# Moving the output stores of a last stage out of the load queue

## The chip, the cores and the metric

The kernel runs on one core of a Trainium2 chip. The metric is the device time of one execution in microseconds (us), the median of three runs. A core has a matrix engine (TensorE, in the profile PE), three elementwise engines (VectorE or DVE, ScalarE or ACT, GpSimd or POOL) and SyncE (SP), which here does nothing but issue DMA transfers. Each engine works through its own instruction stream in order and waits on semaphores. ScalarE can issue DMA transfers too. All transfers between the chip's main memory (HBM) and the on-chip memory (SBUF) are carried out by the same 16 DMA engines of the core.

## The reference

The input `x` has 384 channels of 192 x 192 pixels in float32 (56.6 MB). Two layers, each with a residual, are computed; cut to what matters:

```python
def gn(v):                      # group norm over 32 groups of 12 channels
    ...
def layer0(x):                  # channel attention
    qkv = max_pool_2x2(w_qkv @ x + b_qkv)        # 1152 channels of 96 x 96
    q, k, v = split(depthwise_3x3(qkv) + b_dw)
    attn = normalized(q) @ normalized(k).T       # 8 heads, 48 x 48
    out = sum(a_i * topk_softmax(attn, k_i) @ v) # four values of k
    return w_proj @ repeat_2x2(gelu(out)) + b_proj
def layer1(x):                  # binary convolution with a shift per channel
    xb = sign(x)
    shifted = shift_columns(xb, dx(channel))     # -3 .. 3 columns
    return sign(weight) @ shifted + bias
x = x + layer0(gn(x))
x = x + layer1(gn(x))           # only the sign of gn(x) is needed: x - mean
```

The second layer needs the group means of the whole result of the first, so its pass over the image can start only when the attention of the first layer is done everywhere.

## The kernel before

The image is cut into 24 units of 8 rows (NU = 24), each `[128 partitions, 3 channel tiles, 1536]` float32, 2304 KB. Three passes run over all units: statistics; q and k with their Gram matrix; then v, whose depthwise result stays in six on-chip `chunk` buffers of four units each, with the attention applied in place. The change concerns only what comes after them, the last stage. For every unit it adds the projected attention to `x` in place (`summed`), takes the signs of the result (`signed`, with GpSimd copies that complete the column shifts, `moved`), multiplies them by the sign weights, adds that to `x` in place too and stores the unit (`finished`). Line numbers of the profile stand beside the lines.

```python
def unit(u, pool=big, parts=1):
    xt = pool.tile([P, CT, UPX], F32, name="xt", tag="big")    # CT = 3 channel tiles
    n = CT // parts
    for t in range(0, CT, n):
        nc.sync.dma_start(xt[:, t : t + n], xv[u][:, t : t + n])              # L176
    return xt

def projected(ps, u, m):                # one of three channel tiles
    ...                                 # 6 matmuls on PE                       L493
    for r in range(2):                  # adds them to xt[:, m] in place, DVE   L502
        nc.vector.scalar_tensor_tensor(x5[:, m, r], yb, bpr[:, m : m + 1], x5[:, m, r], ALU.add, ALU.add)

# ... last stage
order = [...]                           # 19, 18, 23, 17, 16, 22, 21, 20, 15, 14, ...
left = [UC] * NCH                       # units that still need each chunk (4 each)
todo = [u for u in order if u not in kept]     # units to load; kept: three are there

def summed(i):
    u = order[i]
    if i >= len(FIRST):                 # the first two were done earlier
        for m in range(CT):
            projected(pyp.tile([P, PPX], F32, name="yps"), u, m)
    left[u // UC] -= 1
    if not left[u // UC] and todo:      # a chunk is done with: its buffer takes a unit
        v = todo.pop(0)
        kept[v] = unit(v, parts=CT)

def signed(i):
    xt, sg = kept[order[i]], signs[i % NSIGN]          # NSIGN = 3
    for t in range(CT):
        for h in range(2):
            ...
            nc.scalar.activation(rows_of(sg, ...), xt[p, t, :]..., AF.Sign, bias=nmean1[...])  # L655
            moved(sg, t, h)             # GpSimd copies                         L633 to L647

def finished(i):
    u = order[i]
    xt, sg = kept.pop(u), signs[i % NSIGN]
    v = todo.pop(0) if todo else None

    def load(m):                        # the next unit, into the same buffer
        if v is not None:
            nc.sync.dma_start(xt[:, m], xv[v][:, m])                          # L673

    for m in range(CT):
        for r0 in range(0, UR, 4):
            ...                         # 6 matmuls on PE                       L680
            nc.vector.scalar_tensor_tensor(blk, ps[...], bl1[...], blk, ALU.add, ALU.add)     # L688
        nc.sync.dma_start(ov[u, :, m], xt[:, m])                              # L691
        if m:
            load(m - 1)
    load(CT - 1)
    if v is not None:
        kept[v] = xt

with tc.manual_schedule():              # instructions go out in this order
    v = todo.pop(0)
    kept[v] = unit(v, more, parts=CT)
    for i in range(3):
        summed(i)
        if i < 2:
            signed(i)
    for i in range(NU):
        if i == 0:
            summed(3)
        elif i > 1 and i + 2 < NU:
            summed(i + 2)
        if i + 2 < NU:
            signed(i + 2)
        finished(i)
```

So SyncE's stream holds, for each unit, store 0, store 1, load 0, store 2, load 1, load 2, each of 768 KB. A load overwrites the third that was just stored, so it waits until that store has landed. At the start of the stage the units have four buffers: eight of the pool less six chunks, and two made for this stage (`early`, `more`). A fifth comes free with the fifth unit, and more as further chunks are done with.

Of the kernel before, what the change touches and what calls it, by code (L numbers as in the profile page):

```python
# [15 lines left out]
AF = mybir.ActivationFunctionType  # L16
# [6 lines left out]
CT = C // P  # L23
# [9 lines left out]
NU = H // UR  # L33
# [9 lines left out]
HALF = P // 2  # L43

STEP = 1584
SAT = [16 + t * STEP + t - SHIFT // 2 for t in range(CT)]
SALL = SAT[-1] + SLEN + PITCH + 9
REST = 32
NSIGN = 3
# [29 lines left out]
def shift_halves():  # L79

    dx = lambda c: (c % SHIFT + SHIFT // 2) % SHIFT - SHIFT // 2
    of = {d: [c for c in range(C) if dx(c) == d] for d in range(-(SHIFT // 2), SHIFT // 2 + 1)}
    shift = [[t - SHIFT // 2, t + 1] for t in range(CT)]
    other = []
    at = np.zeros((P, CT), int)
    for t in range(CT):
        other.append([])
        for h, (d, e) in enumerate(zip(shift[t], (shift[t][1], 0))):  # L90
            n = HALF - len(of[d])
            at[h * HALF : (h + 1) * HALF, t] = of[d][:REST] + of[e][:n] + of[d][REST:]
            of[e] = of[e][n:]
            other[-1].append((e, n))
    assert sorted(at.flat) == list(range(C))
    return at, shift, other


XCH, HSHIFT, OTHER = shift_halves()
# [43 lines left out]
def conv_preact_kernel(ctx: ExitStack, tc: tile.TileContext, a: dict, out: bass.AP):  # L143
    nc = tc.nc
    xv = a["x"].rearrange("u t p n -> u p t n")
    ov = out.rearrange("u t p n -> u p t n")
# [10 lines left out]
    parts = {name: small[:, i:j] for name, i, j in SMALL}  # L157
# [7 lines left out]
    nmean1 = const.tile([P, CT], F32, name="nmean1")  # L165
# [6 lines left out]
    def unit(u, pool=big, parts=1):  # L172
        xt = pool.tile([P, CT, UPX], F32, name="xt", tag="big")
# [4 lines that stand above are left out]
# [36 lines left out]
    kept = {}  # L214
    with tc.tile_pool(name="p1", bufs=1, side="right") as p1, tc.tile_pool(name="p1ps", bufs=2, space=PSUM) as psp:
# [5 lines left out]
        for i in range(NU):  # L221
            u = NU - 1 - i
            xt = unit(u, parts=CT if u in (0, NU - 1) else 1)
# [13 lines left out]
            else:  # L237
                b, k = divmod(seen, BATCH)
# [105 lines left out]
    with tc.tile_pool(name="p2w", bufs=1, side="right") as wp, tc.tile_pool(  # L344
# [7 lines left out]
        for u in range(NU):  # L352
            xt = kept.pop(u) if u in kept else unit(u)
            lo, hi = rows(u)
            n = hi - lo + 1
# [128 lines left out]
    def opened(name, bufs, **kw):  # L484
        return end.enter_context(tc.tile_pool(name=name, bufs=bufs, reuse_waits="tile", **kw))

    def projected(ps, u, m):

        xt = kept[u]
        o = chunk[u // UC][:, :, u % UC * PPX : (u % UC + 1) * PPX]  # L490
        x5 = xt.rearrange("p t (i a j b) -> p t a i j b", a=2, b=2, j=WP)
        for t in range(CT):
            nc.tensor.matmul(  # L493
                ps,
                wpr[:, t, m * P : (m + 1) * P],
                o[:, t, :],
                start=(t == 0),
                stop=(t == CT - 1),
            )
        yb = ps.rearrange("p (i j) -> p i j", j=WP).unsqueeze(3).to_broadcast([P, PR, WP, 2])  # L500
        for r in range(2):
            nc.vector.scalar_tensor_tensor(x5[:, m, r], yb, bpr[:, m : m + 1], x5[:, m, r], ALU.add, ALU.add)  # L502

    chunk = []
    with ExitStack() as vs:
# [39 lines left out]
        for u in range(NU):  # L545
            xt = unit(u)
# [9 lines left out]
            for m in range(CT):  # L556
                parts = []
# [39 lines left out]
    with end:  # L597
        more, sp = opened("p5x1", 1), opened("p5s", 1)
        pyp, psp = opened("p5py", 2, space=PSUM), opened("p5ps", 3, space=PSUM)
        signs = [sp.tile([P, SALL], F8, name=f"signs{i}") for i in range(NSIGN)]  # L600

        rest = [sp.tile([P, SLEN], F8, name=f"rest{i}") for i in range(2)]
        assert SALL % 4 == LEAD % 4 == PITCH % 4 == W % 4 == 0
        for ts in (*signs, *rest):
            nc.gpsimd.memset(ts.bitcast(F32), 0.0)

        def rows_of(ts, p, at=0, pitch=PITCH, n=W):
            return ts[p, at : at + UR * pitch].rearrange("p (r w) -> p r w", w=pitch)[:, :, :n]

        order = [u for c in reversed(range(NCH)) for u in reversed(range(c * UC, (c + 1) * UC))]  # L610
        ahead = [*FIRST, NU - 1, *(u for u in order if u // UC == FIRST[0] // UC and u not in FIRST)]
        order = [*ahead, *(u for u in order if u not in ahead)]
        left = [UC] * NCH
        todo = [u for u in order if u not in kept]

        def summed(i):

            u = order[i]
            if i >= len(FIRST):
                for m in range(CT):  # L620
                    projected(pyp.tile([P, PPX], F32, name="yps"), u, m)
            left[u // UC] -= 1
            if not left[u // UC] and todo:
                v = todo.pop(0)
                kept[v] = unit(v, parts=CT)

        def moved(sg, t, h):

            d, n = OTHER[t][h]
            p = slice(h * HALF + REST, h * HALF + REST + n)  # L630
            src, to = SAT[t] - HSHIFT[t][h], SAT[t] - d
            by = rest[t % 2]
            nc.gpsimd.tensor_copy(  # L633
                rows_of(by.bitcast(I32), p, 0, PITCH // 4, W // 4),
                rows_of(sg.bitcast(I32), p, src // 4, PITCH // 4, W // 4),
            )
            if d:

                assert to % 4 == 0
                nc.gpsimd.tensor_copy(sg.bitcast(I32)[p, to // 4 : (to + SLEN) // 4], by.bitcast(I32)[p])  # L640
            elif to % 2 == 0:
                nc.gpsimd.tensor_copy(
                    rows_of(sg.bitcast(U16), p, to // 2, PITCH // 2, W // 2),
                    rows_of(by.bitcast(U16), p, 0, PITCH // 2, W // 2),
                )
            else:
                nc.gpsimd.tensor_copy(rows_of(sg, p, to), rows_of(by, p))  # L647

        def signed(i):

            xt, sg = kept[order[i]], signs[i % NSIGN]
            for t in range(CT):
                for h in range(2):
                    p = slice(h * HALF, (h + 1) * HALF)
                    nc.scalar.activation(  # L655
                        rows_of(sg, p, SAT[t] - HSHIFT[t][h]),
                        xt[p, t, :].rearrange("p (r w) -> p r w", w=W),
                        AF.Sign,
                        bias=nmean1[p, t : t + 1],
                        saturate=False,  # L660
                    )
                    moved(sg, t, h)

        def finished(i):


            u = order[i]
            xt, sg = kept.pop(u), signs[i % NSIGN]
            v = todo.pop(0) if todo else None

            def load(m):
                if v is not None:
                    nc.sync.dma_start(xt[:, m], xv[v][:, m])  # L673

            for m in range(CT):
                for r0 in range(0, UR, 4):
                    ps = psp.tile([P, 2, 512], F32, name="l1ps")
                    for j in range(2):
                        for t in range(CT):
                            nc.tensor.matmul(  # L680
                                ps[:, j, : 2 * W],
                                wb[:, t, m * P : (m + 1) * P],
                                rows_of(sg, slice(0, P), SAT[t])[:, r0 + 2 * j : r0 + 2 * j + 2],
                                start=(t == 0),
                                stop=(t == CT - 1),
                            )
                    blk = xt[:, m, r0 * W : (r0 + 4) * W].rearrange("p (j n) -> p j n", j=2)
                    nc.vector.scalar_tensor_tensor(  # L688
                        blk, ps[:, :, : 2 * W], bl1[:, m : m + 1], blk, ALU.add, ALU.add
                    )  # L690
                nc.sync.dma_start(ov[u, :, m], xt[:, m])  # L691
                if m:
                    load(m - 1)
            load(CT - 1)
            if v is not None:
                kept[v] = xt

        with tc.manual_schedule():
# [8 lines that stand above are left out]
                    summed(3)  # L707
                elif i > 1 and i + 2 < NU:
                    summed(i + 2)
                if i + 2 < NU:  # L710
                    signed(i + 2)
                finished(i)


# [70 lines left out]
```

## Time and profile before

| | |
|---|---|
| device time, median of three | 2373.09 us (2371.77 to 2376.79) |
| the profiled execution | 2368.62 us, of which the profile spans 2366.8 us |
| PE busy | 2155.2 us, 91% of the span |
| DVE busy | 1825.2 us, 77% |
| ACT busy | 878.2 us, 37% |
| read from HBM, written | 213.68 MB, 56.62 MB |
| share of 16 DMA engines, SyncE's queue | 30.4% |

The profile page is of one execution. It gives the busy time of each engine, the span in 40 slices (a digit is a share in tenths, a last row the GB/s that the DMA engines moved), the chain of work that ended last, groups of instructions with the mean time of one, and the DMA issues with the median time from issue to landing. Answers about a window of time are read in the same way: "windows" gives the busy time of every engine, the number of instructions, the granted clock of PE, the busy share of the DMA engines and their GB/s in each window; "timeline" gives instructions in order of time, merged into runs (start, length, engine, line, operation). A DMA-issuing instruction stands in SyncE's timeline as `SPq`; a run of them includes what they waited for in between. Most of the span, up to about 2012 us, is bound by PE in the three passes and is the same in both kernels; the last 350 us are the stage of the change.

### The profile page before, as it was taken

How to read it: one execution, taken by the hardware profiler on the slowest of the kernel's cores; microseconds unless marked ns; L12 is line 12 of the kernel's file. 1: busy time of each engine (PE TensorE's matmuls, PEld its weight loads, DVE VectorE, ACT ScalarE, POOL GpSimd, SP SyncE). 2: the span in 40 equal slices, each digit the busy share in tenths (PEclk: the TensorE clock that was granted, in tenths of full speed). 3: DMA queues.
4: the chain of work that ended last, by engine and by line, in shares of the span. 5: the costliest groups of instructions: out<-in, count | busy, mean ns of one | idle time of the engine just before them, and what ended most of it. 6: DMA issues, size and time to landing. Idle time of an engine off the chain costs nothing.

```text
span 2366.8 us, 19538 instructions
## 1 busy us (share of the span) xinstructions
PE 2155.2 (91%) x6573; PEld 1029.2 (43%) x6573; DVE 1825.2 (77%) x3113; ACT 878.2 (37%) x1564; POOL 208.5 (9%) x337
## 2 busy tenths in 40 slices
PE   1049999999999999999999999999999999998984
PEld 0024444454444445444444444444444444454542
DVE  4667777777777777777777789986888788898884
ACT  5532222332222322222233222234333332887662
POOL 0000000000000000000000000000000000576552
PEclk7569999999999999999999999999999999999997
DMA  9961111211111111110111023022312222598999
GB/s 399 418 253 40 40 40 41 80 40 41 40 40 41 49 72 40 41 40 0 41 66 54 1 70 120 1 102 100 119 41 82 78 81 80 179 319 294 317 312 379
DMA packets 48596, 271.55 MB, mean 115 GB/s; under 512 B 3408, under 2 KB 4720, under 8 KB 48496
## 3 DMA queue, kind: packets, MB, share of 16 engines
q1 hardware_dynamic: 46704, 266.61, 30.4%
q10 hardware_dynamic: 1792, 3.70, 0.4%
q8 instruction: 51, 0.84, 0.1%
q14 instruction: 49, 0.40, 0.1%
HBM read 213.68 MB, written 56.62 MB: 114 GB/s over the span
## 4 chain that ended last, share of the span: by engine, by line
PE 47%; DVE 33%; ACT 8%; DMA 8%; issue 2%; SPq 0%; POOL 0%; DVEq 0%; ACTq 0%
PE qkv L316 33%; DVE dw L339 18%; DVE pooled L323 9%; DMA xt<-in_x_dram 6%; PE l1ps L680 5%; DVE chunk L339 4%; PE yps L493 3%; ACT pooled L330 3%; ACT dw L337 3%; PE gram L371 3%; DMA out_dram<-xt 2%; PE ops L533 2%; PE tr L367 2%; ACT sq L360 2%; DVE xt L502 1%
## 5 line engine op out<-in xcount | busy, mean ns | idle before, releaser
L316 PE MATMUL qkv<-xt,wq 128*128 128x512 f32 x3888 | 1700.7, 593 | 0.3 <-DVE small L289 0.3
L316 PEld LDWEIGHTS qkv<-xt,wq 128*128 128x128 f32 x3888 | 726.4, 190 | 862.6 <-issue 797.1
L339 DVE SCALAR_TENSOR_TENSOR dw<-pooled,small,dw 128x384 f32<-128x384 f32 (+2 forms) x1152 | 709.8, 616 | 251.3 <-ACT dw L337 226.8
L323 DVE TENSOR_REDUCE pooled<-qkv 128x128 f32<-128x512 f32 x648 | 443.5, 685 | 79.1 <-PE qkv L316 72.7
L339 DVE SCALAR_TENSOR_TENSOR chunk<-pooled,small,chunk 128x384 f32<-128x384 f32 (+3 forms) x696 | 371.2, 548 | 73.4 <-ACT chunk L337 56.0
L341 ACT COPY pooled<-pooled 128x196 f32<-128x196 f32 x207 | 73.7, 356 | 743.4 <-DVE dw L339 520.6
L330 ACT ACTIVATE pooled<-pooled,small 128x384 f32<-128x384 f32 x216 | 133.2, 617 | 332.4 <-DVE pooled L323 332.4
L655 ACT ACTIVATE signs<-xt,nmean 64x1536 fp8e4<-64x1536 f32 x144 | 226.5, 1573 | 74.5 <-DVE xt L502 64.9
L680 PE MATMUL l1ps<-signs,wb 128*128 128x384 fp8e4 x864 | 154.7, 335 | 19.1 <-DVE xt L688 15.4
L502 DVE SCALAR_TENSOR_TENSOR xt<-yps,small,xt 128x768 f32<-128x768 f32 x132 | 128.0, 1013 | 38.6 <-DMA xt<-in_x_dram 22.2
L688 DVE SCALAR_TENSOR_TENSOR xt<-l1ps,small,xt 128x768 f32<-128x768 f32 x144 | 136.1, 1010 | 8.0 <-ACT signs L655 4.0
L493 PE MATMUL yps<-chunk,wpr 128*128 128x384 f32 x396 | 136.5, 491 | 5.8 <-DVE xt L502 5.8
L360 ACT ACTIVATE sq<-dw 128x384 f32<-128x384 f32 (+2 forms) x144 | 75.3, 523 | 158.1 <-DVE dw L339 158.1
L243 DVE BATCH_NORM_STATS2 stats<-xt 128x6 f32<-128x512 f32 x144 | 87.2, 676 | 58.8 <-DMA xt<-in_x_dram 58.8
L297 POOL MEMSET pooled<- 128x196 f32 x9 | 2.4, 265 | 1402.7 <-PE tr L367 1244.8
L680 PEld LDWEIGHTS <-wb 128*128 128x128 fp8e4 x864 | 85.4, 99 | 89.3 <-issue 33.3
L193 PE MATMUL gsps<-sums,small 128*32 128x2 f32 x6 | 0.5, 196 | 126.8 <-DVE sums L264 126.8
L337 ACT ACTIVATE dw<-pooled,small 128x384 f32<-128x384 f32 (+2 forms) x144 | 100.8, 700 | 30.3 <-PE tr L367 28.1
L493 PEld LDWEIGHTS yps<-chunk,wpr 128*128 128x128 f32 x396 | 72.8, 190 | 61.4 <-PE yps L493 17.0
L234 ACT ACTIVATE junk<-xt 128x1536 bf16<-128x1536 f32 x48 | 71.1, 1482 | 52.0 <-DMA xt<-in_x_dram 50.8
L367 PEld LDWEIGHTS tr<-ident,dw 128*128 128x128 f32 (+2 forms) x438 | 52.2, 140 | 70.5 <-DVE dw L339 31.1
L367 PE MATMUL tr<-ident,dw 128*128 128x128 f32 (+2 forms) x438 | 74.3, 279 | 8.9 <-DVE dw L339 8.1
(117 smaller groups left out, 764.0 us busy)
## 6 DMA issues: line engine op xcount, KB each, us to landing
xt<-in_x_dram SPq DMA_DIRECT2D x66, 2304.0 KB, 9.3
out_dram<-xt SPq DMA_DIRECT2D x72, 768.0 KB, 8.9
xt<-in_x_dram SPq DMA_DIRECT2D x69, 768.0 KB, 6.2
wq<-in_w_qkvT_dram ACTq DMA_DIRECT2D x1, 1728.0 KB, 15.4
wl<-in_w_projG_dram ACTq DMA_DIRECT2D x1, 576.0 KB, 3.8
wpr<-in_w_projT_dram ACTq DMA_DIRECT2D x1, 576.0 KB, 5.1
wl<-in_weightT_dram ACTq DMA_DIRECT2D x1, 576.0 KB, 3.8
small<-in_small_dram ACTq DMA_DIRECT2D x1, 110.0 KB, 4.9
```

The lines of the kernel that those rows point to most:

```text
L316: nc.tensor.matmul(ps, wq[:, t, m * P : (m + 1) * P], x4[:, t, r0 : r0 + nr, c0 : c0 + ncol], start=(t == 0), stop=(t == CT - 1),)
L323: nc.vector.tensor_reduce(pl[:, 2 + r0 // 2 : 2 + (r0 + nr) // 2, 1 + c0 // 2 : 1 + (c0 + ncol) // 2], ps.rearrange("p (i a j b) -> p i j ...
L330: nc.scalar.activation(new, new, AF.Identity, bias=bq[:, m : m + 1])
L337: nc.scalar.activation(acc2, src, AF.Identity, bias=bdw[:, m : m + 1], scale=wdw[:, m, 0:1])
L339: nc.vector.scalar_tensor_tensor(acc2, src, wdw[:, m, k : k + 1], acc2, ALU.mult, ALU.add)
L360: nc.scalar.activation(sq[:, : n * WP], acc, AF.Square, accum_out=ssq[:, m, u : u + 1])
L367: nc.tensor.transpose(ps[:L, t * P : (t + 1) * P], dwo[s * CT + t][:, c0 : c0 + L], ident)
L493: nc.tensor.matmul(ps, wpr[:, t, m * P : (m + 1) * P], o[:, t, :], start=(t == 0), stop=(t == CT - 1),)
L502: nc.vector.scalar_tensor_tensor(x5[:, m, r], yb, bpr[:, m : m + 1], x5[:, m, r], ALU.add, ALU.add)
L655: nc.scalar.activation(rows_of(sg, p, SAT[t] - HSHIFT[t][h]), xt[p, t, :].rearrange("p (r w) -> p r w", w=W), AF.Sign, bias=nmean1[p, t : ...
L680: nc.tensor.matmul(ps[:, j, : 2 * W], wb[:, t, m * P : (m + 1) * P], rows_of(sg, slice(0, P), SAT[t])[:, r0 + 2 * j : r0 + 2 * j + 2], sta ...
L688: nc.vector.scalar_tensor_tensor(blk, ps[:, :, : 2 * W], bl1[:, m : m + 1], blk, ALU.add, ALU.add)
```

## The change

It takes the stores out of SyncE's stream and gives them to ScalarE, which issues those of unit `i` between two signs of unit `i + 2`. SyncE is left with the loads, so that a load that waits for a store to land holds up no store. The first three units are still stored and loaded in thirds, the others in one transfer of 2304 KB each way, and so are the units that go into freed chunks. The last two units have no signs after them; their stores remain in SyncE's stream, in thirds. `finished(i)` now stands ahead of `signed(i + 2)` in the program. The orders of instructions on PE, on DVE and on GpSimd are as before, and so are the bytes moved.

```diff
@@ summed
-                kept[v] = unit(v, parts=CT)
+                kept[v] = unit(v)
@@ signed
-            for t in range(CT):
-                for h in range(2):
-                    p = slice(h * HALF, (h + 1) * HALF)
-                    nc.scalar.activation(...)
-                    moved(sg, t, h)
+            for k in range(2 * CT):
+                t, h = divmod(k, 2)
+                p = slice(h * HALF, (h + 1) * HALF)
+                nc.scalar.activation(...)          # the same
+                moved(sg, t, h)
+                if i > 1 and k == min(2 * (i - 2), CT):
+                    stored(i - 2)
@@ finished
-            xt, sg = kept.pop(u), signs[i % NSIGN]
-            v = todo.pop(0) if todo else None
-
-            def load(m):
-                if v is not None:
-                    nc.sync.dma_start(xt[:, m], xv[v][:, m])
-
+            xt, sg = kept[u], signs[i % NSIGN]
             for m in range(CT):
                 ...                                # matmuls and additions, the same
-                nc.sync.dma_start(ov[u, :, m], xt[:, m])
-                if m:
-                    load(m - 1)
-            load(CT - 1)
-            if v is not None:
+                if i + 2 >= NU:
+                    nc.sync.dma_start(ov[u, :, m], xt[:, m])
+
+        def stored(i):
+
+            u = order[i]
+            xt = kept.pop(u)
+            n = 1 if i < CT else CT
+            for t in range(0, CT, n):
+                nc.scalar.dma_start(ov[u][:, t : t + n], xt[:, t : t + n])
+            if todo:
+                v = todo.pop(0)
+                for t in range(0, CT, n):
+                    nc.sync.dma_start(xt[:, t : t + n], xv[v][:, t : t + n])
                 kept[v] = xt
@@ the loop
+                finished(i)
                 if i + 2 < NU:
                     signed(i + 2)
-                finished(i)
```

More of the change, by code (lines that the diff above doesn't have):

```diff
@@ L651, in signed @@
             xt, sg = kept[order[i]], signs[i % NSIGN]
-            for t in range(CT):
-                for h in range(2):
-                    p = slice(h * HALF, (h + 1) * HALF)
[L655 to L661, printed above, removed]
-                    moved(sg, t, h)
+            for k in range(2 * CT):
+                t, h = divmod(k, 2)
+                p = slice(h * HALF, (h + 1) * HALF)
+                nc.scalar.activation(
+                    rows_of(sg, p, SAT[t] - HSHIFT[t][h]),
+                    xt[p, t, :].rearrange("p (r w) -> p r w", w=W),
+                    AF.Sign,
+                    bias=nmean1[p, t : t + 1],
+                    saturate=False,
+                )
+                moved(sg, t, h)
+                if i > 1 and k == min(2 * (i - 2), CT):
+                    stored(i - 2)
         def finished(i):
             u = order[i]
-            xt, sg = kept.pop(u), signs[i % NSIGN]
-            v = todo.pop(0) if todo else None
-            def load(m):
-                if v is not None:
-                    nc.sync.dma_start(xt[:, m], xv[v][:, m])
+            xt, sg = kept[u], signs[i % NSIGN]
             for m in range(CT):
```

## The prediction

> **What bounds the kernel now.** I read the page's slices first. Up to slice 33 PE is at 9 tenths and the DMA row is low; that part is the same in both kernels. From about 2050 us the DMA row is at 9, while PE stays high. So I cut the end into windows of 10 us (columns: the window, its length, PE, PEld, DVE, ACT and POOL busy us with instruction counts, PE's granted clock, DMA share, GB/s).
>
> ```profile
> 2120.00:2130.00 10.00, 9.81 (x43) 5.54 (x41) 8.09 (x10) 7.02 (x6) 6.11 (x11) 1.00 1.00 373
> 2140.00:2150.00 10.00, 9.99 (x50) 5.79 (x49) 9.06 (x11) 8.64 (x6) 7.42 (x12) 1.00 0.84 268
> 2180.00:2190.00 10.00, 6.61 (x33) 3.50 (x32) 7.67 (x9) 7.13 (x5) 7.04 (x11) 0.87 0.78 258
> 2250.00:2260.00 10.00, 6.42 (x32) 3.31 (x30) 6.69 (x8) 7.02 (x5) 6.84 (x11) 0.83 0.76 239
> 2270.00:2280.00 10.00, 8.20 (x37) 4.58 (x36) 9.48 (x11) 6.12 (x5) 6.28 (x9) 1.00 1.04 356
> 2330.00:2340.00 10.00, 8.26 (x51) 4.65 (x48) 9.27 (x10) 0.00 (x0) 0.00 (x0) 1.00 1.02 425
> 2340.00:2350.00 10.00, 0.00 (x0) 0.00 (x0) 0.00 (x0) 0.00 (x0) 0.00 (x0) 0.55 1.01 424
> ```
>
> Two things are to be seen. Nothing computes after 2340 us: the last 27 us are stores alone, at 424 GB/s. And in the middle, with loads and stores mixed, the rate swings between 239 and 373; over the 26 windows from 2060 to 2320 it averages 311 GB/s. The engines could move more than they were given. SyncE's timeline says why.
>
> ```profile
> 2094.04 0.86 SPq L691 DMA_DIRECT2D out_dram<-xt  x2
> 2100.72 0.34 SPq L673 DMA_DIRECT2D xt<-in_x_dram  x1
> 2101.11 0.42 SPq L691 DMA_DIRECT2D out_dram<-xt  x1
> 2102.81 6.25 SPq L673 DMA_DIRECT2D xt<-in_x_dram  x2
> 2109.15 0.86 SPq L691 DMA_DIRECT2D out_dram<-xt  x2
> ...
> 2315.71 35.73 SPq L691 DMA_DIRECT2D out_dram<-xt  x24
> ```
>
> A unit takes 15.1 us of SyncE (2094.04 to 2109.15): two stores go out, then some 6 us pass until the first has landed and load 0 may overwrite it, then store 2, then another 6 us for load 2. Meanwhile finished data waits behind the blocked load. The last line shows the debt: at 2315.7 us the stores of eight units (24 thirds) are still to be issued, though DVE has finished 21 units, so that five lie ready and wait. SyncE's waits and DVE's give the sums (us in total, times, longest):
>
> ```profile
> SPq L673 <- DMA out_dram<-xt: 217.3, 48, 11.3
> DVE xt L502 <- DMA xt<-in_x_dram: 22.2, 15, 2.5
> ```
>
> So 217 of about 270 us of SyncE's stream are loads waiting for stores to land, and 22 us of it reach DVE, and with it PE.
>
> The compute pace, from the chain of waits (start, us, what), is what could remain:
>
> ```profile
> 2060.31 1.95 PE yps L493 x6
> ...
> 2072.62 1.95 PE yps L493 x6
> ...
> 2084.93 1.95 PE yps L493 x6
> ```
>
> 12.31 us a unit, with PE full and DVE with 12 additions of 1.01 us nearly so. Neither order changes, so this pace is a floor.
>
> **What the Trainium skill says.** The page "DMA: Bandwidth & Descriptors", section "Issuing engines are not separate DMA queues", holds that transfers from SyncE and ScalarE run on the same 16 engines, and that several issuers save only sequencer time. I take that as a warning that two queues bring no bandwidth; but here SyncE's time is the 217 us of waits, not the 0.34 us of an issue, and that is what is saved. The same page, "Anatomy of one DMA", gives a transfer a fixed part of about 2 us, mostly the receipt of the write. The trace agrees in kind: the fastest store of 768 KB took 3.3 us to land, and 768 KB at 424 GB/s is 1.85 us, so some 1.5 us are fixed; with one or two thirds in flight that share is lost. "Queues, rings and completion order" says that each DMA engine takes packets in turn from the queues that have work. No mixed two-queue stretch is in this trace; I use it to expect that a load and a store in flight together each get about half. "Perfetto Trace Analysis", section "DMA Optimizations", suggests giving loads and stores to different issuers, as done here.
>
> **The change part by part.**
>
> *Removed:* SyncE's alternation. A store no longer stands behind a load that waits. Nothing of its 217 us is work.
>
> *Added on ACT:* 9 store issues in thirds and 19 whole ones. An issue on SyncE took 0.38 us (median), one on ACT of 1728 KB 0.45 us: 28 x 0.45 = 13 us of ACT. ACT has six signs of 1.57 us a unit, 9.6 of 12.31 us, so 0.45 us a unit fits. ACT also waits for the additions of unit i. Counting from T0, where DVE begins unit i + 2: the timeline has the six L688 of unit i end at T0 + 11.8; signs start at T0 + 2.1 and four of them end at T0 + 8.5, so ACT stands 3.3 us, issues, and the last two signs end near T0 + 15.5. The copy that follows takes 1.5 us: T0 + 17. PE needs these signs two units on, after its L493, at about T0 + 28.9 (2 x 12.31 + 4.3). They have 12 us to spare, and ACT catches up (3.2 + 6.4 = 9.6 us before the next store, which is ready only after 12.3). This costs nothing.
>
> *Moved later:* the first stores. In the trace the signs of unit 1 end at 2049.5 us, and store 0 now follows one sign later, at 2051.1, where it was issued at 2045.5. Store 1 comes after five more signs and three of unit 3, near 2065 (before: 2056.9 to 2064). Unit 5, loaded behind it in thirds, is there by about 2075, and is needed at 2074.6 to 2078.6. I put 0 to 3 us on this.
>
> *Made coarser:* whole units. Store and load in series, each sharing the engines, take (2.36 MB at half of 365 GB/s = 12.9 us) + 1.5, twice: 29 us. With five buffers a unit's buffer has two periods, 24.6 us, between its store and its next use (units 7 to 9); with six it has 36.9. So some 4 us of stall a unit may appear early, 5 to 10 us in all, and none later.
>
> *The sum, by compute:* the last L493 group starts at 2312.26 us (i = 21). At 12.31 us a unit from 2060.31 (i = 2) it would start 19 x 12.31 = 233.9 us later, at 2294.2. The stalls before are thus 18.1 us. The last L688 ends at 2339.3; without them at 2321.2. Units 21, 22 and 23 become storable from about 2311 on: 7.08 MB at 424 GB/s is 16.7 us, plus 1.5: 2329. That is the best case, 38 us below the span before.
>
> *The sum, by bytes:* the windows after 2050 us add up to 102.5 MB, the same after the change. Those in which several transfers were queued and mixed reached 373, 356, 349 (from 2200) and 360 (from 2290) GB/s. I take 365 for a queue kept full: 281 us, so 2331. In the first 60 us with four or five buffers I keep some 320 GB/s as before: 60 x 45 / 365 = 7 us more, 2338, and 2 us for the last landing. **Span 2340 us.** The median lay 6.3 us above the profiled span (2373.1 against 2366.8), so **2346 us**, 27 us (1.1%) less.
>
> **The rivals.** (a) *Compute takes over:* two queues mix at the 424 GB/s of either kind alone. For it: those windows are single direction at full share. Against: mixed windows at share 1.00 to 1.04 gave 356 to 373 only. It gives 2329 + 6 = 2335. (b) *The mixed rate stays:* engine share is already 0.92 on average there, so 311 / 0.92 = 338 GB/s may be all that mixing allows, whoever issues. 102.5 MB then take 303 us: span 2355, median 2361. (c) *A new wait:* whole units with five buffers, store and load in series, stall PE by 4 us in more units than I count, or late first stores delay units 4 and 5; ACT, stopped at a store, hands its delay to the signs. 20 us of it would cancel most of the gain: 2365 to 2375. Against it stand the 12 us of slack on ACT and the growing number of buffers.
>
> **Range and chances.** My value lies between (a) and (b); the range is 2332 to 2364, from the best case to a little above (b). Over 2% faster means under 2325.6, a span of about 2319, below the last L688 without any stall: chance 0.02. Over 2% slower would need 47 us of new stalls: 0.02. Within 2%: 0.96.
>
> **What would show it.** In the profile after: windows from 2110 to 2300 us at about 365 GB/s (338 says rival b, over 400 rival a); stores alone at the end for 8 to 15 us instead of 27; the L502 waits for loads down from 22 us to 5 or 10, and early, before about 2140; ACT waiting some 3 us a unit at stores while PE does not wait for signs. The prediction is wrong if PE starts to wait for ACT or GpSimd in the last stage, if L502 waits over 20 us for loads, or if the part before 2012 us moves by more than the runs scatter (5 us).

## The result, and the profile after

The change takes the kernel from 2373.31 to 2334.21 us (medians of four runs each, the three given above and one more), a ratio of 0.9833, 95% interval 0.9816 to 0.985. Measured again later, beside the last experiments, it came to 2333.66 us against 2369.22, ratio 0.9845 (0.9831 to 0.986). The profiled span is 2331.7 us (before: 2366.8).

Windows of 10 us of the changed kernel, the first four at times that were shown of before (columns as there: window, length, PE, PEld, DVE, ACT, POOL busy, granted clock, DMA share, GB/s):

```profile
2120.00:2130.00 10.00, 7.44 (x26) 4.24 (x25) 6.99 (x8) 5.96 (x5) 5.49 (x9) 0.91 1.02 392
2140.00:2150.00 10.00, 9.80 (x48) 5.34 (x47) 9.52 (x11) 9.44 (x6) 7.17 (x11) 1.00 1.02 426
2180.00:2190.00 10.00, 9.99 (x49) 5.74 (x48) 9.06 (x10) 7.16 (x6) 7.31 (x10) 1.00 1.01 423
2250.00:2260.00 10.00, 9.80 (x45) 5.36 (x44) 9.06 (x11) 9.04 (x6) 6.51 (x10) 1.00 1.01 424
2280.00:2290.00 10.00, 9.80 (x48) 5.55 (x46) 9.48 (x11) 7.16 (x6) 6.61 (x11) 1.00 0.34 139
2320.00:2330.00 10.00, 3.45 (x22) 1.84 (x19) 4.46 (x5) 0.00 (x0) 0.00 (x0) 0.80 0.99 405
```

Loads and stores together now run at 423 to 426 GB/s in three of these windows, as fast as the stores alone did at the end of the kernel before; from 2110 to 2260 us they average 413. PE is full from 2140 us until the last units. From 2280 to 2290 us the DMA engines are idle for two thirds of the time: all loads are done and no debt of stores is left. VectorE's last additions, before and after:

```profile
2322.28 17.04 DVE L688 SCALAR_TENSOR_TENSOR xt<-l1ps,small,xt 128x768 f32<-128x768 f32 x18
```

```profile
2318.62 5.88 DVE L683 SCALAR_TENSOR_TENSOR xt<-l1ps,small,xt 128x768 f32<-128x768 f32 x6 [1.22 <-issue]
```

They end at 2339.3 and 2324.5 us, so the stores alone take 7.2 us at the end instead of 27.

The waits, first of SyncE's stream, then of VectorE (us in total, times, longest):

```profile
SPq L700 <- DMA out_dram<-xt: 219.4, 21, 29.3
DVE xt L502 <- DMA xt<-in_x_dram: 4.6, 3, 2.9
```

The first line is the one to learn from. SyncE's loads still wait 219 us for stores to land, where before it was 217. That wait was never shortened; it only has nothing behind it any more but other loads. What VectorE feels of it fell from 22.2 to 4.6 us.

ScalarE's timeline, around two stores of a whole unit (start, us, engine, line, operation; in brackets the idle time before and its releaser):

```profile
2152.38 9.56 ACT L655 ACTIVATE signs<-xt,nmean 64x1536 fp8e4<-64x1536 f32 x6 [2.70 <-PE yps L493]
2164.18 0.38 ACTq L696 DMA_DIRECT2D out_dram<-xt  x1
2164.69 9.56 ACT L655 ACTIVATE signs<-xt,nmean 64x1536 fp8e4<-64x1536 f32 x6 [2.74 <-PE yps L493]
2176.49 0.38 ACTq L696 DMA_DIRECT2D out_dram<-xt  x1
```

The six signs of a line are two of one unit and four of the next. Then ACT stands about 2.7 us until the last addition of the unit to be stored is done (VectorE's run of six ended at 2164.15), issues the store, and goes on. The bracket names PE, but the store that stands between the two runs of signs went out 0.03 us after that addition. The issue takes 0.38 us.

Where the 35.1 us of span come from: the end of the last addition moved from 2339.3 to 2324.5 (14.8 us), and the stores after it shrank from 27.5 to 7.2 (20.3 us). The medians differ by 39.1 us, 4 more, because the profiled execution of the kernel before was 4.7 us faster than its median and that of the kernel after only 0.7.

### The profile page after: what moved, and what is told of

The parts are those of the page before. It is cut to its first block, busy times and chain, and to the rows that moved or that the text cites. A ratio compares the mean times of both kernels' runs of the same rounds, so it can differ in the third digit from the quotient of the medians.

```text
span 2331.7 us, 19363 instructions
## 1 busy us (share of the span) xinstructions
PE 2154.3 (92%) x6573; PEld 1028.9 (44%) x6573; DVE 1824.6 (78%) x3113; ACT 878.3 (38%) x1564; POOL 209.3 (9%) x337
## 4 chain that ended last, share of the span: by engine, by line
PE 48%; DVE 34%; ACT 9%; DMA 7%; issue 2%; SPq 0%; ACTq 0%; POOLq 0%; POOL 0%; DVEq 0%
PE qkv L316 34%; DVE dw L339 18%; DVE pooled L323 9%; DMA xt<-in_x_dram 6%; PE l1ps L675 5%; DVE chunk L339 4%; PE yps L493 3%; ACT pooled L330 3%; ACT dw L337 3%; PE gram L371 3%; PE ops L533 2%; PE tr L367 2%; DVE xt L502 2%; ACT sq L360 2%; ACT signs L655 1%
## 5 line engine op out<-in xcount | busy, mean ns | idle before, releaser
L493 PE MATMUL yps<-chunk,wpr 128*128 128x384 f32 x396 | 138.2, 495 | 6.7 <-DVE xt L502 6.7
L493 PEld LDWEIGHTS yps<-chunk,wpr 128*128 128x128 f32 x396 | 73.4, 192 | 62.8 <-PE yps L493 16.4
## 6 DMA issues: line engine op xcount, KB each, us to landing
xt<-in_x_dram SPq DMA_DIRECT2D x83, 2304.0 KB, 13.4
out_dram<-xt ACTq DMA_DIRECT2D x19, 2304.0 KB, 13.8
```

The costliest lines, as they stand in the source:

```text
L493: nc.tensor.matmul(ps, wpr[:, t, m * P : (m + 1) * P], o[:, t, :], start=(t == 0), stop=(t == CT - 1),)
```

## The experiments

Two theories stood at the start. *Blocked stream:* in SyncE's single in-order stream a load that waits for a store to land holds up the next stores; nothing else goes out meanwhile, the DMA queue runs dry, and the order costs more than 12.3 us a unit. *Size* and *two rings* are the rivals: larger transfers, or reads and writes from two queues, would let the DMA engines mix the two kinds faster. Most of the runs below can be read from one number, the GB/s from 2110 to 2260 us, which is pure last stage in all of them. Here is that window, first of the kernel before and the kernel after:

```profile
2110.00:2260.00 150.00, 135.07 (x590) 75.08 (x589) 124.69 (x133) 104.72 (x67) 92.92 (x135) 0.98 0.90 302
```

```profile
2110.00:2260.00 150.00, 145.25 (x641) 81.24 (x640) 134.63 (x143) 112.86 (x72) 98.30 (x143) 0.99 1.01 413
```

### e1: two issuers, everything in thirds

```diff
 # on the change
-                kept[v] = unit(v)
+                kept[v] = unit(v, parts=CT)
@@ stored
-            n = 1 if i < CT else CT
+            n = 1
```

Expected: 

> The change with all stores and loads in thirds of 768 KB, issuers as in the change. Theory 'blocked stream' (in SyncE's stream a store stood behind loads that waited for two landings per unit in turn, 15.1 us against a compute pace of 12.3): the issuers are what counts, 2332 to 2340 us, mixed windows over 400 GB/s. Rival 'size' (transfers of 2304 KB raise the rate of mixed traffic, the two issuers little): back to 2355 to 2373, mixed windows about 320 to 350 GB/s. A third reading, 'shared semaphores': all transfers take eight semaphores in turn, with six transfers a unit a store must wait for the transfer eight issues earlier, so ScalarE is held up: 2340 to 2355 with ACT waiting on DMA.

Measured: 2327.53 us, ratio to before 0.9807 (0.9787 to 0.9827), 420 GB/s in the window:

```profile
2110.00:2260.00 150.00, 147.60 (x656) 82.55 (x654) 138.34 (x146) 113.27 (x72) 98.40 (x142) 1.00 1.02 420
```

The transfers are as small as before and the rate is there: *size* is out. It is even faster than the change, by some 6 us, and below the range I had given. The third reading fits the trace but does little harm. The transfers' landings are counted on eight semaphores, 26 or 27 transfers on each. At 2106.22 us a run of three stores took 8.39 us of ScalarE's stream, some 4.7 of them after the unit's last addition (2109.9), and the next signs began 7.1 us late; PE did not wait for them.

### e2: one issuer, whole units

```diff
 # on the kernel before; from the fourth unit on
-                nc.sync.dma_start(ov[u, :, m], xt[:, m])
-                if m:
-                    load(m - 1)
-            load(CT - 1)
+            nc.sync.dma_start(ov[u], xt)
+            if v is not None:
+                nc.sync.dma_start(xt, xv[v])
```

(The last two units are stored in thirds, and freed chunks are loaded whole, as in the change.)

Expected: 

> The kernel before with one 2304 KB store and one load a unit from the fourth unit on, all still in SyncE's stream (store, then the load of the same buffer). 'Blocked stream': one landing a unit of 8 to 13 us instead of two in turn, which fits or nearly fits 12.3 us: 2336 to 2350. 'Size': the same as the change, 2334. Rival 'two rings' (the DMA engines mix reads and writes at 424 GB/s only when these come from two queues): mixed windows stay at 340 to 370 and the time at 2355 or more.

Measured: 2361.29 us, ratio 0.9954 (0.9931 to 0.9976). A miss: my theory had promised 2336 to 2350, and *two rings* had said 2355 or more. (*Size*, with 2334, missed too.) The window, and SyncE's timeline, show what I had sized wrongly:

```profile
2110.00:2260.00 150.00, 136.34 (x604) 76.26 (x602) 127.22 (x135) 104.57 (x67) 93.75 (x135) 1.00 0.87 327
```

```profile
2155.76 1.59 SPq L698 DMA_DIRECT2D out_dram<-xt  x1
2169.88 0.37 SPq L700 DMA_DIRECT2D xt<-in_x_dram  x1
2170.34 0.44 SPq L698 DMA_DIRECT2D out_dram<-xt  x1
2184.70 0.37 SPq L700 DMA_DIRECT2D xt<-in_x_dram  x1
2185.12 0.48 SPq L176 DMA_DIRECT2D xt<-in_x_dram  x1
```

There is one landing a unit as intended, but a whole store lands 14.9 us (median) after its issue, not 8 to 13. It is issued 0.46 us behind a whole load in the same queue (2169.88 and 2170.34), and the 4.7 MB of the two alone take an estimated 11.1 us at 424 GB/s. The cycle is 14.6 us (2155.76 to 2170.34), again over 12.3. So e2 could not tell *blocked stream* from *two rings*; the next three can.

### e3: one issuer, thirds, loads one unit later

```diff
 # on the kernel before; from the fourth unit on no load in the unit's own turn, but
+            if i >= CT:
+                if stored and todo:
+                    w, old = todo.pop(0), stored.pop(0)
+                    for m in range(CT):
+                        nc.sync.dma_start(old[:, m], xv[w][:, m])
+                    kept[w] = old
+                stored.append(xt)
```

Expected: 

> The kernel before in thirds and in SyncE's stream alone, but from the fourth unit on the loads into a buffer are issued after the stores of the next unit, so that the store they wait for has landed by then. 'Blocked stream': SyncE hardly waits for stores, 2336 to 2346 (the loads come some 5 us later, which may stall some early units). 'Size' and 'two rings': no gain, 2360 to 2375.

Measured: 2325.69 us, ratio 0.9806 (0.9782 to 0.9829): the whole gain and some more, 10 us under the range I had given, with nothing moved off SyncE. The same window and SyncE's largest waits, in e3:

```profile
2110.00:2260.00 150.00, 143.17 (x623) 79.81 (x623) 131.72 (x140) 108.48 (x70) 95.48 (x138) 0.98 1.02 421
```

```profile
SPq L691 <- DVE xt L688: 139.4, 58, 25.9
SPq L673 <- DMA out_dram<-xt: 38.0, 9, 9.7
...
SPq L701 <- DMA out_dram<-xt: 11.7, 8, 2.7
```

One queue mixes reads and writes at 421 GB/s; *two rings* is out as well. SyncE now waits for VectorE to finish data (139 us), which is what a stream of stores should wait for. Its loads wait 11.7 us for landings from the fourth unit on (L701) and 38.0 for the first three (L673), where I left the old order. The three dots stand for two lines, 22.1 and 19.7 us of waits for earlier loads to land, which neither theory called for; PE's pace shows no trace of them outside the one stall that follows. The late loads cost one stall of 5.0 us, at 2115 us, in the profiled execution, which was the slowest of the four (2332.3; the others 2324.3 to 2326.0).

### e4: one issuer, thirds, three stores and then three loads

```diff
 # on the kernel before
-                if m:
+                if m and i < CT:
                     load(m - 1)
-            load(CT - 1)
+            for m in range(CT - 1 if i < CT else 0, CT):
+                load(m)
```

Expected: 

> The kernel before in thirds and in SyncE's stream alone, but from the fourth unit on the order is store 0, 1, 2, load 0, 1, 2 instead of store 0, 1, load 0, store 2, load 1, 2: one wait for a landing a unit instead of two in turn. 'Blocked stream': about 8 us of wait between the last store of a unit and the first of the next, which come 8 us apart: 2338 to 2352. 'Size' and 'two rings': 2360 to 2375.

Measured: 2334.7 us, ratio 0.9840 (0.9817 to 0.9864). Only the order of six issues is different from before, and the median is the change's.

```profile
2110.00:2260.00 150.00, 147.60 (x657) 82.74 (x655) 138.22 (x147) 113.38 (x73) 101.51 (x146) 1.00 0.98 376
```

A wait of 7 to 11 us is left in each cycle (stores from 2121.66 to 2123.3 us, loads from 2134.59; the next at 2140.5 and 2147.38). Thirteen cycles, from 2095.34 to 2278.18, take 14.1 us each, against 17.1 in the kernel before (2094.04 to 2315.71) and a compute pace of 12.31. So loads come in time and PE is full (147.6 of 150 us), but stores still gather, and 11.8 us of them follow the last addition (2318.6 to 2330.4).

### e11: one issuer, whole units, loads one unit later

The order of e3 with the transfers of e2.

```diff
 # on e2
                 nc.sync.dma_start(ov[u], xt)
-                if v is not None:
-                    nc.sync.dma_start(xt, xv[v])
+            if i >= CT:
+                if stored and todo:
+                    w, old = todo.pop(0), stored.pop(0)
+                    nc.sync.dma_start(old, xv[w])
+                    kept[w] = old
+                stored.append(xt)
```

Expected: 

> As e2 (2304 KB transfers, SyncE's stream alone), but the load into a buffer stands behind the store of the next unit, as in e3. 'Blocked stream' says that e2 failed because its one wait a unit (11 to 14 us for a whole store to land behind a whole load) was again longer than 12.3 us with the rest: without it 2328 to 2340, mixed windows over 400 GB/s. If whole transfers in one stream are slow for another reason, it stays near e2's 2361.

Measured: 2335.64 us, ratio 0.9854 (0.9839 to 0.9869), and 411 GB/s in the window against e2's 327:

```profile
2110.00:2260.00 150.00, 140.78 (x612) 78.55 (x611) 129.40 (x138) 106.38 (x69) 93.91 (x136) 0.97 1.01 411
```

Moving the load behind the next store undid e2's failure: it was the wait, not whole transfers in one queue. Two things make it slower than e3: one early stall of 7.4 us (unit 8, at 2117.6), where e3 has one of 5.0 at the same unit; and stores of 8.1 us after the last addition, where e3 has 4.4. That a whole store and a whole load must follow each other in one buffer would explain the longer stall; no run separates that.

### e5: whole units from the start

```diff
 # on the change
-            n = 1 if i < CT else CT
+            n = CT
```

Expected: 

> The change with the first three units stored and loaded whole as well. Few buffers early: unit 4 then lands about 2063 us and unit 5 about 2078 to 2082, for uses at 2061 and 2074. 'Turnaround of a buffer' (a whole store and then a whole load are too long while there are four buffers): 6 to 12 us of L502 waits for loads before 2090 us, 2341 to 2347. Rival (the thirds of the first three units are of no use): 2334.

Measured: 2338.55 us, ratio 0.9858 (0.9841 to 0.9875), some 4 to 5 us over the change. Load waits of VectorE come to 6.9 us, of 3.51, 1.05 and 2.38, at units 4, 5 and 7. Its four runs (2337.3 to 2340.2) lie above all nine of the change (2332.0 to 2336.5). The thirds of the first three units are worth having; I had put them at 7 us or more.

### e6 and e7: the stores near the end, and the place amid the signs

e6 stores the last six units from SyncE in thirds, as each third is finished; no loads remain there to be in the way.

```diff
 # e6, on the change; LATE = NU - 6
-                if i + 2 >= NU:
+                if i >= LATE:
                     nc.sync.dma_start(ov[u, :, m], xt[:, m])
@@ stored
+            if i >= LATE:
+                return
 # e7, on the change
-                if i > 1 and k == min(2 * (i - 2), CT):
+                if i > 1 and k == (min(2 * (i - 2), CT) if i < 2 + CT else 2 * CT - 1):
```

Expected of e6: 

> The change with the stores of the last six units in SyncE's stream, in thirds as each is finished, where no loads remain. It takes away the whole store of the fourth last to third last units from ScalarE, with it the wait of the last two signs, and lets unit 21 go out in thirds: the gap of 1.2 us before the last six additions goes and the stores end sooner: 2 to 3 us less, 2331 to 2332. If the end is set by the bytes queued by then alone, no difference (2334).

Expected of e7: 

> The change with each store from the sixth unit on after the last sign of the unit two further, not after the fourth. If the place amid the signs matters only through the wait of the last signs, the stores go out at the same moment (when the last addition is done), ACT's 2.7 us of idle time a unit stay without effect, and the last unit gains its 1.2 us: 2332 to 2335. Rival (the place amid the signs was chosen because later ones delay stores and so loads): stores about 3 us later, stalls at units 8 to 10 grow, 2337 or more.

Measured: e6 2328.61 us (ratio 0.9815, 0.9797 to 0.9833), e7 2333.64 (0.9836, 0.9819 to 0.9853). In the changed kernel VectorE stands 1.22 us before the last six additions, because the last two signs wait behind the store of unit 21; in both e6 and e7 its last 18 additions run without that gap. This line is e7's:

```profile
2305.89 17.04 DVE L683 SCALAR_TENSOR_TENSOR xt<-l1ps,small,xt 128x768 f32<-128x768 f32 x18
```

Yet e7 gains nothing that can be told from scatter: its stores after the last addition take 8.5 us in place of 7.2. The end hangs on the whole store of unit 21. It is issued at 2311.88 us in the change and at 2311.56 in e7, the DMA engines have nothing to move just before (share 0.00 from 2310 to 2312 in both), and both spans end 19.8 us later. So the gap, to which I had given 1.2 us, cost nothing that shows. e6, some 3 us better than I had expected, stores that unit in thirds, so that its first can leave four additions, some 3.7 us, earlier; there the stores after the last addition take 4.4 us. Its early load waits were also 2.1 us instead of 4.6, which the edit does not touch and which I put down to scatter.

e7 moves the whole stores, those of the fourth unit on, behind the last sign of the unit two further. Nothing is lost by that either: the stores go out when the data is ready in both places, so their place amid the signs matters little.

### e9 and e10: the version that is faster than both, and what it leaves

e9 is e1 with the last eight units stored by SyncE. e10 is e9 without the loads into stored buffers: 16 units are then computed on old data, so its time says only what compute and stores need.

```diff
 # e9, on e1; LATE = NU - 8
-                if i + 2 >= NU:
+                if i >= LATE:
                     nc.sync.dma_start(ov[u, :, m], xt[:, m])
@@ stored
+            if i >= LATE:
+                return
 # e10, on e9
-                for t in range(0, CT, n):
-                    nc.sync.dma_start(xt[:, t : t + n], xv[v][:, t : t + n])
                 kept[v] = xt
```

Expected of e9: 

> Candidate to beat all: two issuers, everything in thirds (as in e1, 2327.5), and the stores of the last eight units, after which there are no loads, in SyncE's stream as each third is finished. 'Thirds shorten the turnaround, and the waits of ScalarE at stores cost only at the end': 1 to 2 us under e1, 2325 to 2327. If ScalarE's waits at the stores cost nothing at all: 2327.5.

Expected of e10: 

> The variant of e9 with the loads into stored buffers left out (16 of the units are then computed on old data; four loads into freed chunks stay, all stores stay). It measures what the compute of the last stage and the final stores need when no load can be late. 'Compute has taken over': 2322 to 2326, at most 3 us under e9. If transfers still hold the variants of the change up elsewhere: 2315 or less.

Measured: e9 2326.18 us, ratio 0.9805 (0.9789 to 0.9821); e10 2325.12, ratio 0.9809 (0.9794 to 0.9823). Here is the window of e9 and then of e10:

```profile
2110.00:2260.00 150.00, 147.60 (x657) 82.90 (x656) 138.21 (x147) 114.73 (x73) 100.22 (x145) 1.00 1.01 414
```

```profile
2110.00:2260.00 150.00, 147.61 (x657) 82.91 (x656) 138.20 (x146) 116.41 (x74) 102.12 (x149) 1.00 0.60 236
```

In e10 the DMA engines move 236 GB/s in place of e9's 414 and are busy 0.60 of the time, PE is just as full, and the time is the same within about a microsecond. So e1, e3 and e9 (ratios 0.9807, 0.9806 and 0.9805) stand, within the scatter, at what compute and the last stores allow for this order; they can't be told apart. The repeated run of the change itself had this on record:

> The change itself once more, beside the others on one chip, for the comparison with e9 and e3: 2332 to 2336.

It came to 2333.66 us, with e10 and e11 and on another chip than e3 and e9. Compared by the ratios to the kernel before (0.9845 and, the first time, 0.9833, against 0.9805 and 0.9806), e9 and e3 are some 7 to 9 us faster than the change.

The reordering of `finished` and `signed` in the program, by itself, leaves the instruction order of every engine as it was in the kernel before, so it had no run; e3 and e4 gain without it.

## Why the prediction was right, and which term was off

*The bound of the kernel before and the mechanism* were right; what I took to bound the kernel after, the bytes, was not. I had named the blocked loads of SyncE as the cause, the debt of stores at the end and the stalls as the two places of the gain. Both shrank: the stalls to 4.6 us of load waits, the stores at the end to 7.2 us. e3 and e4 (against the kernel before) and e11 (against e2) show the cause by changing nothing but the order of issues.

*The direction and the range* held, but the value of 2346 us was 12 us too high. The term that failed is the mixed rate in "the sum, by bytes", which made the span 8.3 us too long (2340 against 2331.7): I took 365 GB/s for a queue kept full, from the fullest mixed windows of before (349 to 373). Measured are 413 in the change, 420 in e1 and 421 in e3, nearly as for one direction. With 413 the same sum ends at an estimated 2307 us (2050 + 102.5 MB at 413 GB/s + 7 + 2), before the sum by compute, so that the bytes no longer set the end. Those windows had looked full, at a DMA share of 0.99 to 1.04, and were not. The error was to read that share as capacity used; rival (b), with rate divided by share (338), made the same error more strongly, and the 302 GB/s at share 0.90 before against 413 at 1.01 after refute it. The other 3.8 us are the step from the span to the median: I added 6.3 us, measured are 2.5. The time is 1.8 us above the span in both profiled executions; the rest of the 6.3 was a profiled execution of before that happened to be fast.

Rival (a), compute takes over, was the right one. That its 2335 comes so near the measured 2334.21 is partly luck: its span of 2329 was 2.7 us too short, and the same 6.3 us made up for it.

*The sum by compute* held. It put the last addition without any stall at 2321.2 us and the end at 2329. Measured: 2324.5 and 2331.7, with 4.6 us of load waits left. The sum was itself some 2 us too long, since it took two load waits of 0.80 and 1.34 us in the last unit before (at 2317.14 and 2320.42) for compute. With most loads left out (e10), the last addition ended at 2319.2 and the span at 2323.9.

*Stalls of 5 to 10 us before 2140 us* were 4.6 us, at units 5, 6 and 9, in the stretch with few buffers; the largest, 2.88 us at 2126 us, is followed by another 2.18 us on PE. The 29 us that I gave a whole store and a whole load in series were about right: their median landings are 13.8 and 13.4 us. e1 shows that thirds all the way avoid most of it: one wait of 1.7 us.

*ACT at no cost* held: 2.7 us of idle a unit, predicted 3.3. At the end, where the last unit has no later one to hide behind, VectorE did wait, 1.22 us, but e7 ended no earlier without that gap. PE's waits for GpSimd's sign copies went from 3.5 to 4.5 us by it; this is the sign of being wrong that I had named, at a size that cost nothing that shows.

*That two issuers bring no bandwidth of their own*, as the Trainium skill's page "DMA: Bandwidth & Descriptors" has it in "Issuing engines are not separate DMA queues", agrees with the runs: 420 GB/s from two issuers, 421 from one. What the second issuer saved here was the wait of stores behind loads, and a new order in one stream saved it too.

*Store 0 at 2051.1 us* was wrong: it was issued at 2044.89, when only ten of the thirteen signs ahead of it had begun. It went out no later than before (2045.5), and the thirds of store 1 went out from 2055.5 to 2060.5, against 2056.9 to 2064.1 before. Unit 5, loaded behind store 1, still made VectorE wait 1.16 us at 2078.7, within the 0 to 3 us I allowed, although the first stores went out no later.

*Rival (c), whole units stall more*, was real but small. The profiled spans of the change and of e1 differ by 7.9 us: 1.5 lie before the fifth unit's L493 group (it starts at 2059.23 and 2057.76), which the edit does not touch; 3.6 lie between that group and the last addition, where the stalls are, and 2.8 are stores after it.

## What to carry to other kernels

In an in-order stream of transfers, look at what stands behind each wait, not at the length of the wait: the change left 219 us of waits in SyncE's stream and still gained 39, because nothing urgent stood behind them. The cheapest cure may be the order in the one stream, issuing a load after the next unit's store, so that what it waits for has already happened (e3), before a second issuer is brought in. Take the rate that the DMA engines could reach from a stretch where work is surely queued, such as a drain at the end, and not from the busy share of a stretch where the issuer waits. Here the stores alone, at 424 GB/s, were within 3% of what mixed traffic reached (413 to 421).

## What the runs showed of the hardware

- Reads and writes mixed moved 420 GB/s from two issuers (e1) and 421 from one (e3), in transfers of 768 KB; 413 in the change, mostly in 2304 KB. Stores alone had reached 424 to 425.
- At the same busy share of about 1.0 the engines moved 356 GB/s (before, 2270 to 2280 us) or 426 (after, 2140 to 2150). Within the changed kernel, windows of 10 us at 1.00 to 1.02 range from 377 to 428. The share says that packets were under way, not that no more would have fitted.
- ScalarE issued a transfer while signs ahead of it in its program were still to run: store 0 at 2044.89 us, after ten signs from 2029.73 on, though thirteen stand ahead of it. This line and its neighbours, from ScalarE's timeline of the changed kernel:

```profile
2029.73 15.96 ACT L655 ACTIVATE signs<-xt,nmean 64x1536 fp8e4<-64x1536 f32 x10 [5.30 <-issue]
2044.89 0.37 ACTq L696 DMA_DIRECT2D out_dram<-xt  x1
2045.72 1.57 ACT L655 ACTIVATE signs<-xt,nmean 64x1536 fp8e4<-64x1536 f32 x1
```

- A store of 2304 KB landed 14.9 us after its issue in one queue with loads of the same size (e2, median), and 13.8 us beside loads from another issuer (the change, median). At 424 GB/s its bytes take 5.6 us.
